# Block-contiguous rows, paired one-hot comparison and shared gather tiles for sixteen ranges in a two-layer graph network

## The chip, the cores and the metric

The kernel runs on one core of one Trainium2 chip. The metric is device time in microseconds (us); a run's time is that of the core, and the kernel before took 14195.87 us, the median of three runs (14195.01 to 14202.4). About 0.2% is what a measurement of this kernel can tell from no change.

## The reference

There are 32768 nodes with 128 features and 524288 edges, sorted by destination. Layer 0 sums neighbours, attends inside groups of 512 nodes, and passes a small network with batch norms. Layer 1 makes three rounds; each sums neighbours again. Cut to what matters here:

```python
# layer 0
agg = jax.ops.segment_sum(x[src], dst, num_segments=N)
h = (1.0 + eps) * x + agg
h = relu(h @ W_loc1 + b_loc1) @ W_loc2 + b_loc2
h_local = _bn(x + h, g1, beta1)
...                                  # attention of 64 groups x 512 nodes, 8 heads of 16
h = h_local + _bn(x + o, g2, beta2)
f = relu(h @ Wf1 + bf1) @ Wf2 + bf2
x = _layernorm(x + _bn(h + f, g3, beta3))
# layer 1, three times (row = src, col = dst)
attn = softmax(x @ Wq.T @ keys.T)    # 512 keys
norm_x = dinv[:, None] * x
agg = zeros_like(x).at[row].add(norm_x[col])
lap = x - dinv[:, None] * agg
x = 0.5 * x + 0.5 * (attn @ values - 0.2 * lap)
# then layer norms and the output
```

The cost lies in the four neighbour sums: one in layer 0 and three in layer 1. Each sends one row of 128 values along each of 524288 edges.

## The kernel before, in words

**Ranges, slots, overflow.** The nodes are cut into 256 ranges of 128 (`NW`). Between each pair of ranges there are `KS = 6` slots for edges. A neighbour sum has two halves. In the first half the sending range multiplies its rows by a one-hot matrix `pick` and so places each row into its slot (`Exchange.spread`, L1406-L1419: matmul `exp`, copy to `y_o` by ScalarE or VectorE, DMA to `slots`). In the second half the receiving range loads its slots (`y_i`, L1424), builds a one-hot matrix `oh` of 19 column groups on VectorE (`Exchange.hot`, L1438-L1442), and adds 19 matmuls into one PSUM tile (`Exchange.add`, L1453). Values are carried as three bf16 parts of 128 each, a row of 384 bf16 elements (768 bytes; 772 bytes in layer 0's table, which has two more columns).

Edges that find no slot are the overflow. Per range, `OW = 5` tiles of 128 rows are gathered by GpSimd with indirect DMAs from the table `rows` (`listed`, L1429), with row numbers from the tensor `other`. What overflows these goes to `SH = 2` tiles of gathered rows shared by `GW = 8` ranges (`common`, L1429 too, asked for at L1434 when `i % GW == 0`, row numbers from `shared`). So one neighbour sum issues 256 x 5 + 32 x 2 = 1344 indirect DMAs of 128 rows. If an overflow did not fit, a flag would lead to a general path (`layer0_any`, `layer1_any`) that is not run here.

**Stages**, with where they lie in the profile:

- Attention of layer 0 (0 to about 3530 us). VectorE also sorts the edges and builds the tensors `slot`, `other`, `shared`, `row` in pieces between attention steps (`Grid.build` L543, `Grid.build_more` L809). The loop at L2122 gives these pieces a quota of 3.35 us of declared cost (`SHARE`) per attention step; each `yield` declares the cost of a piece.
- First half of layer 0's sum (L1741-L1749, about 3530 to 4530 us).
- Second half of it together with the network of `local` (L1802, 4533 to 6235 us). The order is written out by hand (`manual_schedule`). `Sums` (L1455) asks for the gathers and slots six ranges ahead, in seven buffers, and builds one-hots two ahead.
- The second network (L1841, to about 6490 us).
- First half of layer 1's first sum with its softmax (L2039-L2056, about 6490 to 7960 us).
- Two rounds in which each block of four ranges has both the second half of one sum and the first half of the next (L2063-L2082, 7969 to about 10198 us, and on to about 12470 us). `Sums` there builds its one-hots one ahead and compares with `gc["iota1"]`, which lies in SBUF.
- The last second half with the final layer norms (L2086-L2096, 12477 to 14199 us), again in an order by hand. Here and in layer 0's second half `oh` compares with a copy of the ramp in PSUM (`ramp_in_psum`, L1320), in fp32.

**Block tensors.** `rows_of(t, i)` (L1316) views a block of 512 nodes as `[128, 4, d]`: partition `p` holds nodes `p`, `128 + p`, `256 + p`, `384 + p`. A DMA of a block of fp32 features thus moves pieces of 512 bytes, and one of the table `rows` pieces of 768. It is used for the inputs and the output, for the table (`end`, L1361), for `part_d` (what a round adds to the sum: written at L1958, read at L1984), and for `x_d` of round 0 (written at L1891, read at L1988).

**One-hots.** At L1440 the slot number of each of 19 columns is one bf16 element, repeated 128 times along the row by a step of 0, compared with a ramp of 128.

Of the kernel before, what the change touches and what calls it, by code (L numbers as in the profile page):

```python
# [10 lines left out]
I32 = mybir.dt.int32  # L11
# [18 lines left out]
KS = 6  # L30
OV = 6
OW = 5
GW = 8
SH = 2
WL = 2304
BIN = 1024
# [372 lines left out]
                                ordt.rearrange("p t c -> p (t c)"))  # L409


class Grid:


# [128 lines left out]
    def build(self, pp):  # L543
# [9 lines left out]
        with tc.tile_pool(name="gr", bufs=1) as sp:  # L553
# [13 lines left out]
            for h in range(2):  # L567
                with tc.tile_pool(name=f"gr_h{h}", bufs=1) as hp:
# [89 lines left out]
                    with tc.tile_pool(name=f"gr_c{h}", bufs=1) as ap:  # L658
# [19 lines left out]
                        for t, n in ((0, 3), (3, OW - 3)):  # L678
# [5 lines left out]
                        nc.vector.tensor_scalar(key, lw, OS, 7, op0=OP.logical_shift_right,  # L684
                                                op1=OP.logical_shift_left)
                        yield two / 3
                        nc.vector.tensor_scalar(m, lw, main.oth, P - 1, op0=OP.logical_shift_right,
                                                op1=OP.bitwise_and)
                        yield two / 3
                        nc.vector.tensor_tensor(m, m, key, OP.bitwise_or)  # L690
                        yield one / 3
                        nc.vector.tensor_copy(fb[:, :OL], m)
                        yield two / 3
                        nc.vector.tensor_tensor(fb[:, :OL], fb[:, :OL], valid, OP.mult)
# [114 lines left out]
    def build_more(self, lane, pp):  # L809
# [12 lines left out]
        with tc.tile_pool(name="mo", bufs=1) as sp:  # L822
# [10 lines left out]
            for h in range(2):  # L833
                word = words[h]
                m = sp.tile([P, L], I32, name="m")
                n = sp.tile([P, L], I32, name="n")
                valid = sp.tile([P, L], F32, name="valid")
                val = sp.tile([P, L], F32, name="val")
                sz = sp.tile([P, 1], F32, name="sz")
                w = sp.tile([P, 1], F32, name="w")  # L840
                nc.vector.tensor_scalar(w, over.lane_f, float(h * P + 2), None, op0=OP.add)
                nc.vector.tensor_scalar(m, word, over.WSHIFT, None, op0=OP.logical_shift_right)
                yield L / 1000
                nc.vector.tensor_scalar(valid, m, w, None, op0=OP.is_equal, op1=OP.add, accum_out=sz)
# [13 lines left out]
                yield L / 1000  # L858
                nc.vector.tensor_scalar(m, m, 7, None, op0=OP.logical_shift_left)
                yield L / 1000  # L860
                nc.vector.tensor_scalar(n, word, over.oth, P - 1, op0=OP.logical_shift_right, op1=OP.bitwise_and)
                yield L / 1000
                nc.vector.tensor_tensor(m, m, n, OP.bitwise_or)
                yield L / 1000
                nc.vector.tensor_tensor(val, m, valid, OP.mult)
                yield L / 1000
                for t, c in ((0, 3), (3, OW - 3)):
                    yield from self.turned(pp, [val[:, (t + j) * P:(t + j + 1) * P] for j in range(c)],
                                other[:, h, :, t:t + c].rearrange("e w t -> e t w"))
                yield from self.share(pp, sp, keys, val[:, OW * P:OL], sz, self.bad[:, self.NBAD - 2 + h:self.NBAD - 1 + h],  # L870
                           slot[:, OW:, h, :], shared[:, h])
# [18 lines left out]
def tile_gnn_resnorm(ctx: ExitStack, tc: tile.TileContext, a: dict, out: bass.AP):  # L890
# [417 lines left out]
    def grid_consts(pool):  # L1308
        gc["iota1"] = pool.tile([P, P], BF16, name="iota1")
        nc.vector.tensor_scalar(gc["iota1"], iota, 1.0, None, op0=OP.add)  # L1310
        gc["lane1"] = pool.tile([P, 1], F32, name="lane1")
        nc.vector.tensor_scalar(gc["lane1"], lane_f, 1.0, None, op0=OP.add)
        gc["ident"] = pool.tile([P, P], BF16, name="ident_b")
        nc.vector.tensor_copy(gc["ident"], ident)

    def rows_of(t, i):  # L1316

        return t.rearrange("(b c p) d -> b p c d", c=NCH, p=P)[i]

    def ramp_in_psum(pool):  # L1320

        t = pool.tile([P, P], F32, name="ramp_p")
        nc.vector.tensor_copy(t, gc["iota1"])
        return t

    class Exchange:
# [14 lines left out]
            nc.sync.dma_start(self.row.rearrange("p h f -> p (h f)"), self.grid["row"])  # L1341

        def load_tables(self, pool):
            self.slot = pool.tile([P, NC2, NW], BF16, name="slot")
            nc.sync.dma_start(self.slot.rearrange("p c w -> p (c w)"), self.grid["slot"])
            self.other = pool.tile([P, NW, OW], I32, name="other")
            nc.scalar.dma_start(self.other.rearrange("p w c -> p (w c)"), self.grid["other"])
            self.shared = pool.tile([P, NW // GW, SH], I32, name="shared")
            nc.scalar.dma_start(self.shared.rearrange("p g c -> p (g c)"), self.grid["shared"])

        def split_steps(self, wp, b, x, rest):
# [6 lines left out]

            def end():
                nc.vector.tensor_sub(r[:, :, 2, :], rest, r[:, :, 1, :])  # L1360
                nc.sync.dma_start(rows_of(self.table, b), t)  # L1361
            return t[:, :, :ROW], [lambda: nc.scalar.copy(r[:, :, 0, :], x),
                                   lambda: nc.vector.tensor_sub(rest, x, r[:, :, 0, :]),
                                   lambda: nc.scalar.copy(r[:, :, 1, :], rest), end]
# [72 lines left out]

        def hot(self, wp, i, ramp, bufs):  # L1438
            oh = wp.tile([P, NC2, P], BF16, name="oh", bufs=bufs)
            nc.vector.tensor_tensor(oh, ramp[:, None, :].to_broadcast([P, NC2, P]),  # L1440
                                    self.slot[:, :, i].unsqueeze(2).to_broadcast([P, NC2, P]), OP.is_equal)
            return oh  # L1442

        def add(self, ps, oh, got, k):
# [412 lines left out]
    def layer1_grid(v_d, s3, c3):  # L1857

        exs = [Exchange("src", slots_d[t % 2], rows_d[t]) for t in range(T_STEPS)]
        with tc.tile_pool(name="l1g", bufs=1) as gp:  # L1860
# [9 lines left out]
            def first(b, st, wp, p_tr):  # L1870
# [17 lines left out]

                def norm():
                    layer_norm(wp, st["x0"], st["x"])  # L1890
                    nc.sync.dma_start(rows_of(xs_d[0], b), st["x"])  # L1891
                return load, [(7, scale), (12, turn), (15, norm)]

            def prepare(t, b, st, wp, p_s, p_tr):
# [25 lines left out]
            def emit(t, b, st, wp, p_e, p_s, p_tr, share):  # L1920
# [30 lines left out]
                def remain():  # L1951
# [3 lines left out]
                    part = wp.tile([P, NCH, D], F32, name="part_o")  # L1955
                    nc.vector.tensor_tensor(part, ps, st["rec"].unsqueeze(2).to_broadcast([P, NCH, D]), OP.mult)
                    nc.vector.scalar_tensor_tensor(part, st["x"], 0.4, part, op0=OP.mult, op1=OP.add)
                    nc.sync.dma_start(rows_of(part_d, b), part)  # L1958

                def spread(n):  # L1960
                    c, m = divmod(n, KS)
# [18 lines left out]
            def ask_part(t, b, wp):  # L1980

                if b < NB:
                    p_i = wp.tile([P, NCH, D], F32, name="part_i", bufs=3)
                    nc.scalar.dma_start(p_i, rows_of(part_d, b))  # L1984
                    parts[b] = [p_i]
                    if t == T_STEPS - 1:
                        x1 = wp.tile([P, NCH, D], F32, name="x1", bufs=3)
                        nc.scalar.dma_start(x1, rows_of(xs_d[0], b))  # L1988
                        parts[b].append(x1)

            def consume(t, b, st, sums, wp, extra=()):
# [186 lines left out]
```

## Time and profile before

| what | value |
|---|---|
| runs: median of 3 | 14195.87 us |
| the profiled execution: its own time / its span | 14201.3 us / 14199.4 us |
| busy: PE (matmul) / VectorE (DVE) / ScalarE (ACT) / GpSimd (POOL) | 12173.8 / 11413.1 / 6658.1 / 6079.5 us |
| one-hots `oh` with the ramp in PSUM | 512 of 2681 ns |
| one-hots `oh` with the ramp in SBUF | 512 of 2683 ns |
| indirect DMAs `listed` / `common` | 5120 of 1118 ns / 256 of 1299 ns |
| shortest and median of all indirect DMAs | 941 and 946 ns |
| copies `y_o` on ACT / DVE | 4224 of 808 ns / 1920 of 954 ns |
| DMA in all | 3602.99 MB in 1640075 packets |

The busy time of PE is modelled and holds pipelined matmuls twice over in part. Idle time of POOL that is put down to "issue" is time for which the profile shows nothing to wait for. The share of the DMA is the mean over the core's 16 DMA engines; as packets of different queues can overlap on an engine, it can pass 1.

### The profile page before, as it was taken

Reading aid. Unit: us, or ns where it says so; the run is one execution under the profiler, and the core shown is the slowest. Engines: PE = TensorE matmul, PEld = TensorE weight load, DVE = VectorE, ACT = ScalarE, POOL = GpSimd, SP = SyncE. Lnnn points to the kernel's source line nnn. Section 1 sums busy time; section 2 is a strip of 40 time slices with the busy share of each in tenths; the row PEclk is TensorE's granted clock in tenths of the full one; section 3 lists DMA queues with packets and bytes.
Section 4 is the critical chain, followed back from the end, with each engine's and each line's share of the span. In section 5 each row is a group of like instructions: output and inputs, shape, how many; then the busy total and the mean of one; then the engine's idle time right before and its main releaser. Section 6 shows DMA issues by size and latency. Waiting matters only on the chain. (4 is left out here: it accounts for less than half of the span.)

```text
span 14199.4 us, 168166 instructions
## 1 busy us (share of the span) xinstructions
PE 12173.8 (86%) x58982; PEld 5828.9 (41%) x58982; DVE 11413.1 (80%) x16677; ACT 6658.1 (47%) x10316; POOL 6079.5 (43%) x5461
## 2 busy tenths in 40 slices
PE   8888888889887888888998799999899999966666
PEld 3232223333333444444444355555455555533333
DVE  7998998776998888877888677777677777778888
ACT  4343444334987111127888566666566666610000
POOL 0000000000001777740000477877688878767777
PEclk9898888888999999999999999999999999987787
DMA  1000000000999999977888899999999999988887
GB/s 40 11 11 17 10 11 12 18 8 33 348 346 348 309 309 309 310 242 261 304 311 308 299 383 385 390 383 383 350 376 386 382 391 381 383 292 285 286 283 256
DMA packets 1640075, 3602.99 MB, mean 254 GB/s; under 512 B 199346, under 2 KB 976466, under 8 KB 1638066
## 3 DMA queue, kind: packets, MB, share of 16 engines
q1 hardware_dynamic: 1165424, 2936.81, 55.6%
q0 software_dynamic: 258752, 533.02, 12.3%
q10 hardware_dynamic: 215042, 122.32, 2.8%
q8 instruction: 465, 7.62, 0.2%
q14 instruction: 392, 3.21, 0.1%
HBM read 2088.45 MB, written 1503.00 MB: 253 GB/s over the span
## 5 line engine op out<-in xcount | busy, mean ns | idle before, releaser
L1429 POOL DMA_INDIRECT listed<-rows,other x5120 | 5725.6, 1118 | 3544.2 <-issue 3151.1
L1416 ACT CAST y_o<-exp 128x768 bf16<-128x768 f32 x4224 | 3224.0, 808 | 1271.9 <-DMA slots<-y_o 627.2
L1411 PE MATMUL exp<-rows,pick 128*128 128x384 bf16 x12288 | 2768.2, 326 | 394.9 <-ACT y_o L1416 289.4
L1453 PEld LDWEIGHTS <-oh 128*128 128x128 bf16 x19456 | 1992.2, 102 | 2648.8 <-issue 1629.8
L1453 PE MATMUL seg<-y_i,oh 128*128 128x384 bf16 x12288 | 2745.0, 349 | 9.3 <-DMA y_i<-slots 9.3
L1416 DVE CAST y_o<-exp 128x768 bf16<-128x768 f32 x1920 | 1830.9, 954 | 687.4 <-PE exp L1411 636.2
L1411 PEld LDWEIGHTS <-pick 128*128 128x128 fp8e4 x12288 | 1185.1, 97 | 2115.5 <-issue 1550.7
L1453 PE MATMUL seg<-listed,oh 128*128 128x384 bf16 (+1 forms) x5120 | 1257.6, 336 | 815.5 <-DMA listed<-rows,other 777.2
L1606 ACT ACTIVATE pT<-s 128x1024 f32<-128x1024 f32 x1024 | 1021.5, 1023 | 1353.7 <-PE s L1602 1351.3
L1586 DVE TENSOR_REDUCE mx<-s 128x2 f32<-128x1024 f32 x1024 | 1204.4, 1219 | 270.5 <-PE s L1580 270.2
L1440 DVE TENSOR_TENSOR oh<-ramp_p,slot 128x2432 bf16<-128x2432 f32 x512 | 1372.3, 2681 | 12.7 <-DMA slot<-slot_dst 9.4
L1440 DVE TENSOR_TENSOR oh<-iota,slot 128x2432 bf16<-128x2432 bf16 x512 | 1373.7, 2683 | 3.0 <-DMA slots<-y_o 3.0
L283 POOL DMA_INDIRECT c_r<-pivots_over,c_ix x2 | 1.9, 946 | 3056.7 <-DVE c_ix L281 3056.4
L1602 PE MATMUL s<-ql,k 32*128 32x512 f32 x4096 | 1032.4, 692 | 259.2 <-DVE mx L1586 244.6
L2005 DVE SCALAR_TENSOR_TENSOR part_i<-seg,dinv,part_i 128x128 f32<-128x128 f32 x1536 | 529.6, 345 | 543.0 <-PE seg L1453 531.9
L1064 ACT ACTIVATE ln_rs<-ln_mv,eps_c 128x4 f32<-128x4 f32 x192 | 57.1, 297 | 1670.8 <-DVE ln_mv L1062 1489.7
L1930 PE MATMUL s<-keysT,qT 128*128 128x512 f32 x1536 | 818.2, 615 | 7.3 <-ACT pr L1043 3.7
L1453 PE MATMUL seg<-common,oh 128*128 128x384 bf16 (+1 forms) x2048 | 600.7, 350 | 194.5 <-DMA common<-rows,shared 194.2
L1942 PE MATMUL s<-pt,values 128*128 128x512 f32 x1536 | 750.6, 600 | 10.8 <-ACT pt L1937 10.6
L1580 PE MATMUL s<-k,q 32*128 32x512 f32 x4096 | 745.2, 726 | 6.0 <-DVE mx L1586 2.6
L1613 PE MATMUL pv<-pT,vx 128*32 128x512 f32 x4096 | 698.6, 751 | 0.2 <-ACT pT L1606 0.2
L1388 PE MATMUL row_p<-row,ident_b 128*128 128x512 bf16 x1536 | 601.8, 392 | 82.9 <-DVE pick L1381 62.3
(393 smaller groups left out, 14180.8 us busy)
## 6 DMA issues: line engine op xcount, KB each, us to landing
slots<-y_o SPq DMA_DIRECT2D x2048, 576.0 KB
y_i<-slots SPq DMA_DIRECT2D x1024, 1152.0 KB
pick<-pick SPq DMA_DIRECT2D x1024, 192.0 KB
listed<-rows,other POOLq DMA_INDIRECT x5120
rows<-rows SPq DMA_DIRECT2D x192, 384.0 KB
part_d<-part_o SPq DMA_DIRECT2D x192, 256.0 KB
part_i<-part_d ACTq DMA_DIRECT2D x192, 256.0 KB
rows<-rows SPq DMA_DIRECT2D x64, 386.0 KB
```

The costliest lines, as they stand in the source:

```text
L1411: nc.tensor.matmul(ps[:, j, :ROW], pick[:, o:o + P], r, start=True, stop=True)
L1416: (nc.vector.tensor_copy if to_dve else nc.scalar.copy)(dst, ps[:, :, :ROW])
L1429: nc.gpsimd.indirect_dma_start(out=g[:, k, :], out_offset=None, in_=self.table, in_offset=bass.IndirectOffsetOnAxis(ap=index[:, k:k + 1], ...
L1440: nc.vector.tensor_tensor(oh, ramp[:, None, :].to_broadcast([P, NC2, P]), self.slot[:, :, i].unsqueeze(2).to_broadcast([P, NC2, P]), OP.is ...
L1453: nc.tensor.matmul(ps[:, :n], oh[:, j, :], src, start=(k == 0), stop=(k == NC2 - 1))
L1580: nc.tensor.matmul(two[s // 2][:, s % 2, :], t["q", o][32 * s:32 * s + 32, c * P:(c + 1) * P], t["k", o][32 * s:32 * s + 32, :], start=Tru ...
L1586: nc.vector.tensor_reduce(m[:, c, 2 * i:2 * i + 2, xr[o]], st[b]["two"][i], AX.X, OP.max, negate=True)
L1602: nc.tensor.matmul(two[s // 2][:, s % 2, :], t["k", o][32 * s:32 * s + 32, c * P:(c + 1) * P], t["ql", o][32 * s:32 * s + 32, :], start=Tr ...
L1606: nc.scalar.activation(t["p", c][:, 2 * i:2 * i + 2, :], two[i], AF.Exp)
L1613: nc.tensor.matmul(t["o"][32 * s:32 * s + 32, :], t["v"][:, c, s, 2 * o:2 * o + 2, :].rearrange("p z e -> p (z e)"), t["p", c][:, s, :], s ...
L1930: nc.tensor.matmul(s, st["q"][:, c * P:(c + 1) * P], keysT, start=True, stop=True)
L1942: nc.tensor.matmul(ps, values[:, k, :], st["pt"][:, k, :], start=(k == 0), stop=(k == NCH - 1))
```

## The change

- `GW` becomes 16: the two shared tiles serve sixteen ranges, so they are asked for 16 times per sum, not 32 times.
- `kept_of(t, i)` stores the four rows that partition `p` of a block's tile holds side by side, as rows `4p` to `4p + 3` of that block of the tensor, so that one partition's part is one contiguous piece. It replaces `rows_of` for the tables `rows`, for `part_d` and for `x_d` of round 0, but not for inputs and output. The row numbers in `other` and `shared` follow the new order: `row_index` computes them, with six operations where two stood.
- `load_tables` loads `slot` into a tile of its own, and two VectorE copies per load turn it into a tensor `[P, NW, NC2, 2]` in which each element stands twice, side by side. It is loaded twice, for layer 0's second half and at the start of layer 1.
- `hot` compares in pairs: the innermost dimension of all three operands has two neighbouring elements.
- The ramp in PSUM becomes bf16, written by a TensorE transpose of `gc["down"]`.

```diff
-GW = 8
+GW = 16
...
+def row_index(nc, dst, spare, window, lane):
+    n = NCH.bit_length() - 1
+    cost = dst.shape[-1] / 1000
+    lane(dst)
+    yield cost
+    nc.vector.tensor_scalar(dst, dst, n, None, op0=OP.logical_shift_left)
+    yield cost
+    nc.vector.tensor_scalar(spare, window, 7, NCH - 1, op0=OP.logical_shift_right, op1=OP.bitwise_and)
+    yield cost
+    nc.vector.tensor_tensor(dst, dst, spare, OP.bitwise_or)
+    yield cost
+    nc.vector.tensor_scalar(spare, window, 7 + n, 7 + n, op0=OP.logical_shift_right, op1=OP.logical_shift_left)
+    yield cost
+    nc.vector.tensor_tensor(dst, dst, spare, OP.bitwise_or)
+    yield cost
...
-                        nc.vector.tensor_scalar(m, lw, main.oth, P - 1, op0=OP.logical_shift_right,
-                                                op1=OP.bitwise_and)
-                        yield two / 3
-                        nc.vector.tensor_tensor(m, m, key, OP.bitwise_or)
-                        yield one / 3
+                        yield from row_index(
+                            nc, m, fb[:, :OL].bitcast(I32), key,
+                            lambda t: nc.vector.tensor_scalar(t, lw, main.oth, P - 1, op0=OP.logical_shift_right,
+                                                              op1=OP.bitwise_and))
...
+        gc["down"] = pool.tile([P, P], BF16, name="down")
+        nc.vector.tensor_copy(gc["down"], gc["lane1"].to_broadcast([P, P]))
...
+    def kept_of(t, i):
+        return t.rearrange("(b p c) d -> b p (c d)", c=NCH, p=P)[i]
...
     def ramp_in_psum(pool):
-        t = pool.tile([P, P], F32, name="ramp_p")
-        nc.vector.tensor_copy(t, gc["iota1"])
+        t = pool.tile([P, P], BF16, name="ramp_p")
+        nc.tensor.transpose(t, gc["down"], gc["ident"])
         return t
...
-            self.slot = pool.tile([P, NC2, NW], BF16, name="slot")
-            nc.sync.dma_start(self.slot.rearrange("p c w -> p (c w)"), self.grid["slot"])
+            self.slot = pool.tile([P, NW, NC2, 2], BF16, name="slot")
+            with tc.tile_pool(name="slot_l", bufs=1) as lp:
+                t = lp.tile([P, NC2, NW], BF16, name="slot_1")
+                nc.sync.dma_start(t.rearrange("p c w -> p (c w)"), self.grid["slot"])
+                for o in range(2):
+                    nc.vector.tensor_copy(self.slot[:, :, :, o], t.rearrange("p c w -> p w c"))
...
-                nc.sync.dma_start(rows_of(self.table, b), t)
+                nc.sync.dma_start(kept_of(self.table, b), flat(t))
...
-            nc.vector.tensor_tensor(oh, ramp[:, None, :].to_broadcast([P, NC2, P]),
-                                    self.slot[:, :, i].unsqueeze(2).to_broadcast([P, NC2, P]), OP.is_equal)
+            nc.vector.tensor_tensor(oh.rearrange("p c (w z) -> p c w z", z=2),
+                                    ramp.rearrange("p (w z) -> p w z", z=2)[:, None].to_broadcast([P, NC2, P // 2, 2]),
+                                    self.slot[:, i].unsqueeze(2).to_broadcast([P, NC2, P // 2, 2]), OP.is_equal)
...
-                    nc.sync.dma_start(rows_of(part_d, b), part)
+                    nc.sync.dma_start(kept_of(part_d, b), flat(part))
...
-                    nc.scalar.dma_start(p_i, rows_of(part_d, b))
+                    nc.scalar.dma_start(flat(p_i), kept_of(part_d, b))
...
-                        nc.scalar.dma_start(x1, rows_of(xs_d[0], b))
+                        nc.scalar.dma_start(flat(x1), kept_of(xs_d[0], b))
```

The same replacement by `row_index` stands in `build_more` (L861-L865), and the same `kept_of` at L1891. `flat` merges the last two dimensions of a tile.

More of the change, by code (lines that the diff above doesn't have):

```diff
@@ L860, in build_more @@
                 yield L / 1000
[L861 to L865, printed above, removed]
+                yield from row_index(
+                    nc, n, val.bitcast(I32), m,
+                    lambda t: nc.vector.tensor_scalar(t, word, over.oth, P - 1, op0=OP.logical_shift_right,
+                                                      op1=OP.bitwise_and))
+                nc.vector.tensor_tensor(val, n, valid, OP.mult)
                 yield L / 1000
@@ L1318, in rows_of, with flat @@
         return t.rearrange("(b c p) d -> b p c d", c=NCH, p=P)[i]
+    def kept_of(t, i):
+        return t.rearrange("(b p c) d -> b p (c d)", c=NCH, p=P)[i]
+    def flat(t):
+        return t.rearrange("p c d -> p (c d)")
     def ramp_in_psum(pool):
-        t = pool.tile([P, P], F32, name="ramp_p")
-        nc.vector.tensor_copy(t, gc["iota1"])
+        t = pool.tile([P, P], BF16, name="ramp_p")
+        nc.tensor.transpose(t, gc["down"], gc["ident"])
         return t
@@ L1890, in norm @@
                     layer_norm(wp, st["x0"], st["x"])
-                    nc.sync.dma_start(rows_of(xs_d[0], b), st["x"])
+                    nc.sync.dma_start(kept_of(xs_d[0], b), flat(st["x"]))
                 return load, [(7, scale), (12, turn), (15, norm)]
```

## The prediction, made before the run

> **What bounds the kernel now.** The time is a chain of stages, so I read busy times by stage first: the stretches of the profile cut at stage borders (columns: stretch, its length, then busy time and instructions of PE, PE's weight loads, DVE, ACT, POOL; the granted clock, the DMA share, GB/s).
>
> ```profile
> 3540.00:4530.00 990.00, 835.23 (x3831) 366.82 (x3828) 924.74 (x1273) 892.27 (x1276) 6.57 (x62) 1.00 0.91 346
> 4543.00:6225.00 1682.00, 1368.94 (x6610) 731.69 (x6611) 1489.59 (x2671) 184.41 (x443) 1270.34 (x1344) 0.93 0.94 308
> 6500.00:7950.00 1450.00, 1299.50 (x5982) 689.35 (x5983) 1250.68 (x2359) 1268.14 (x2100) 0.00 (x0) 0.99 0.85 304
> 7969.00:10160.00 2191.00, 2040.15 (x10341) 1117.96 (x10342) 1577.97 (x2058) 1295.39 (x2148) 1743.74 (x1344) 0.98 1.01 377
> 10198.00:12400.00 2202.00, 2059.41 (x10461) 1129.91 (x10460) 1588.23 (x2077) 1322.41 (x2191) 1747.59 (x1344) 0.99 1.01 379
> 12477.00:14181.00 1704.00, 1096.38 (x4848) 545.10 (x4849) 1381.56 (x2844) 38.73 (x127) 1294.43 (x1344) 0.79 0.86 285
> ```
>
> In the two stages with hand-written order (second and last row) POOL looks only 76% busy. Its order in time says otherwise:
>
> ```profile
> 13299.35 0.95 POOL L1429 DMA_INDIRECT listed<-rows,other  x1 [0.30 <-issue]
> 13300.60 0.94 POOL L1429 DMA_INDIRECT listed<-rows,other  x1 [0.30 <-issue]
> 13301.85 0.95 POOL L1429 DMA_INDIRECT listed<-rows,other  x1 [0.30 <-issue]
> ```
>
> One starts every 1.25 us, 0.95 busy and 0.30 of issue. 1344 x 1.25 = 1680 us, and the stretches are 1682 and 1704 us long: POOL never rests, and it **bounds both stages**. That PE waits 440.6 us there for `listed` (the waits of 12500 to 14100 us) agrees.
>
> In the two rounds (fourth and fifth row) an indirect DMA takes longer:
>
> ```profile
> L1429 POOL DMA_INDIRECT listed<-rows,other x1280 | 1637.4, 1279 | 2171.4 <-issue 2071.2 <-PE seg L1453 54.2 <-PE exp L1411 20.8
> L1429 POOL DMA_INDIRECT common<-rows,shared x64 | 107.0, 1671 | 20.1 <-issue 16.1 <-PE seg L1453 2.8 <-PE exp L1411 1.2
> ```
>
> The timeline shows why, first POOL's and then DVE's:
>
> ```profile
> 9004.28 0.95 POOL L1429 DMA_INDIRECT listed<-rows,other  x1 [0.30 <-issue]
> 9005.53 3.40 POOL L1429 DMA_INDIRECT listed<-rows,other  x1 [0.30 <-issue]
> 9009.23 0.95 POOL L1429 DMA_INDIRECT listed<-rows,other  x1 [0.30 <-issue]
> ```
>
> ```profile
> 9005.42 2.68 DVE L1440 TENSOR_TENSOR oh<-iota,slot 128x2432 bf16<-128x2432 bf16 x1
> ```
>
> A one-hot whose two inputs lie in SBUF holds POOL's instruction until it is done. Over a round that is 1743.7 - 1344 x 0.946 = 472 us. POOL's demand is thus 1680 + 472 = 2152 of 2191 us. But the DMA engines are full too:
>
> ```profile
> q1 hardware_dynamic: 112714, 317.11, 82.3%
> q0 software_dynamic: 29405, 60.29, 16.9%
> q10 hardware_dynamic: 15312, 7.60, 2.6%
> ```
>
> These are the DMA queues from 8500 to 9500 us (packets, MB, share of 16 engines): 101.8% together. Counting in the trace's DMA records how many packets are open at each moment of 8100 to 10100 us, I find 16 or more for 92% of the time and 13 to 15 for most of the rest; in the last stage only 58%. ACT waits 279.4 us (8000 to 10150 us) for a write of `slots` before it may reuse `y_o`. So I hold the **DMA engines for the bound of the rounds**, POOL 2% behind. PE's floor is 88% of a round (start-to-start: 0.162 us for a matmul of 384 columns, 0.43 for a pass of an fp32 one of 512, 0.109 for a transpose).
>
> [...] The records of 8100 to 10100 us agree: 512 B take 27.0 ns (q10: 27.5), 768 B 36.0, 1536 B 65.5, 4608 B 187.0, so about 6 ns plus 25 B/ns.
>
> **The change part by part**, from the profiled execution: its span of 14199.4 us, 14201.3 with what lies around it, 5 us above the median.
>
> *GW = 16.* Each sum loses 32 of 1344 indirect DMAs: 32 x 1.25 = 40 us of POOL. Layer 0's second half and the last stage: **-40 each**, on the path. What is late next there: DMA, 0.94 and 0.86 busy, and DVE, 0.89 and 0.81, which the one-hots relieve. I counted on the inputs that sixteen ranges need at most 173 (by destination) and 180 (by source) of the 256 shared rows, so the general path isn't taken.
>
> *One-hots in pairs.* [...] 1.27 us x 256 = 324 us of DVE per sum. On the path: **0**, for DVE bounds none of the four stages with one-hots; POOL or the DMA covers it. In the rounds POOL's hold shrinks with it, from 472 to 472 x 1415 / 2681 = 249 us; hidden behind the DMA engines. If that cover is gone, a round gets worth more (rival A). If PSUM keeps 2681 ns, nothing changes on the path.
>
> *Rows side by side.* Per block and partition: four packets of 768 B (144 ns) become one of 3072 B (126, between the 1536 and 4608 B rows), and four of 512 B (108 and 110) become one of 2048 B (86), written and read. 18 + 22 + 24 = 64 ns x 128 partitions / 16 engines x 64 blocks = 33 us per round. With 32 fewer gathers (each 202 + 72 + 9 ns per engine: 9 us) 42 us per round on the bound itself. With POOL and DVE relieved, the engines may run a little fuller (20 us windows reach 1.05): I take **-50 each** round, bounds -35 and -85. In layer 1's first half the same saves about 31 us of DMA work, but the engines are at 0.85 and PE, DVE, ACT at 0.86 to 0.90: -5 (0 to -25). In layer 0's first half 772 B rows save 11 us of DMA, with DVE at 0.93: -3 (0 to -11).
>
> *Loading the slots.* Two copies of 256 x 19 = 4864 bf16, read 512 B apart and written 4 B apart. No row shows one. [...] In layer 0's second half (from 4533 us) slots land at 4540.5, and the first gather starts at 4542.7; behind the copies on DVE stand the first one-hots, behind these PE. PE may start late, since POOL has seven buffers (37 gathers, 46 us) to fill. [...] buffers laid over the loading tile wait: **+8** (0 to 20). At the start of layer 1 (6490 us) DVE's next work is at 6501, and PE, ACT, DVE are all near full after it: **+10** (0 to 20).
>
> *`row_index`.* Per half three more `tensor_scalar` and one more `tensor_tensor`: for 768 columns 3 x 0.54 + 0.95 (scaled from 943 to 1351 and 1749 to 2547 ns for 1536 and 2304) = 2.6 us, for 896 columns 2.9; twice each, 11 us of DVE in the attention stage. There a group of 512 takes 39 us without sorting work and 50 to 75 with it (times between `stats_w`), so DVE is on the path: of DVE's 2946 us in the stage the attention's own rows sum to 1556, and the other 1390 lengthen it by 3530 - 64 x 39 = 1034 us. 11 x 0.74 = **+8** (0 to 15). The declared costs rise by 14 us, or four steps of about 9 us; sorting ended at 3374 of 3530 us, so there is room.
>
> *The new ramp*: two transposes; 0.
>
> Sum: -40 + 8 (layer 0's second half), -3, -5 + 10, -50 - 50, -40, +8 = **-162**; 14201.3 - 162 = 14039, and against the median **14034**.
>
> **The rivals.** *A: the rounds are bound by POOL, not the DMA.* For: POOL idles only 38 us beyond its issue gaps in a round. Against: packets are always queued. POOL's floor would be 1640 + 249 = 1890, PE's about 1950; the fullest 20 us windows move 411 GB/s, and 823 MB at that rate take 2002 us: -189 each in place of -50. 14034 - 278 = **13756**.
>
> *B, slower: the faster one-hot holds POOL also with the ramp in PSUM.* At 2681 ns it doesn't (945 ns per gather), [...] no trace shows the paired mode. If it held POOL as the SBUF form does (0.69 of its length), 0.98 us x 256 = 250 us in each of two POOL-bound stages: 14034 + 500 = **14534**. It decides from a hold of 0.32 us per one-hot (162 / 512).
>
> *C: POOL's bound gives way to the next one.* If in both POOL-bound stages landing gathers take over halfway (-20 each), the rounds gain only 25 each and loads cost 20 each: -20 -20 -25 -25 +40 +8 -3 -5 = -50, **14146**.
>
> *D: the pairs don't engage.* DVE keeps its 2681 ns, and the forecast stays: **14034**, as it rests on POOL and DMA.
>
> **How the numbers follow.** Forecast (with D) 0.67, A 0.10, B 0.07, C 0.16. Forecast's own range: 13950 to 14100. Leaving out A and B and a tail: 13930 to 14150. Faster by over 0.2% (28 us, about what this kernel's measurement can tell from no change): forecast, A and most of C, 0.90; same 0.03; slower B and a bad C, 0.07.
>
> **What would show it.** `common` x128 in all; indirect DMAs still 1.25 us apart in the hand-ordered stages, which shrink by about 40 us; `oh` near 1415 ns in SBUF, 1415 or 2681 in PSUM; long gathers near 1.9 us, not 3.4; rounds 50 us shorter with a DMA share still above 1; packets of 3072 and 2048 B near 126 and 86 ns. I am wrong if rounds shrink by over 100 us, if gathers in the hand-ordered stages pass 1 us, or if a load of slots costs over 20 us.

## The result and the profile after

The changed kernel took 13944.75 us, the median of four runs (13941.91 to 13967.72); the kernel before took 14197.09 us beside it. The ratio is 0.982 with a 95% interval of 0.9807 to 0.9834: 252 us less, where 162 were forecast. The profiled execution took 13967.7 us (span 13965.9), 233.6 us less than that of before and 23 us more than its own median. Cut at the same events in both traces, near the end of each stage, the stages are:

| stage | before, us | after, us | difference | forecast |
|---|---|---|---|---|
| attention with the sorting | 3530 | 3533 | +3 | +8 |
| layer 0, first half | 999 | 994 | -6 | -3 |
| layer 0, second half | 1702 | 1669 | -33 | -32 |
| second network | 257 | 260 | +3 | 0 |
| layer 1, first half | 1475 | 1488 | +13 | +5 |
| round 1 | 2235 | 2143 | -92 | -50 |
| round 2 | 2272 | 2185 | -88 | -50 |
| last second half | 1729 | 1695 | -34 | -40 |

The stretches of the kernel after, with the columns that the prediction explains (length; busy time and instructions of PE, weight loads, DVE, ACT, POOL; clock, DMA share, GB/s):

```profile
3540.00:4527.00 987.00, 837.58 (x3837) 367.61 (x3836) 926.70 (x1277) 892.05 (x1277) 6.63 (x62) 1.00 0.90 348
4538.00:6190.00 1652.00, 1348.52 (x6618) 719.55 (x6619) 1203.72 (x2675) 184.49 (x443) 1246.80 (x1312) 0.95 0.93 312
6467.00:7930.00 1463.00, 1299.96 (x5982) 689.81 (x5983) 1257.11 (x2361) 1269.37 (x2100) 0.00 (x0) 0.99 0.83 302
7949.00:10040.00 2091.00, 2002.48 (x10324) 1123.74 (x10325) 1268.54 (x2055) 1295.02 (x2145) 1382.11 (x1312) 0.99 1.02 393
10122.00:12196.00 2074.00, 1996.62 (x10317) 1120.38 (x10316) 1269.69 (x2057) 1297.12 (x2149) 1353.28 (x1284) 1.00 1.02 396
12277.00:13946.00 1669.00, 1096.07 (x4848) 544.55 (x4849) 1065.49 (x2848) 38.73 (x127) 1267.47 (x1312) 0.80 0.85 289
```

In the second and last row POOL now has 1312 indirect DMAs instead of 1344. At 1.25 us each they are 1640 us, and the stretches are 12 and 29 us longer than that (before 2 and 24 us longer than 1680): POOL still bounds both. Its order in time in the last stage is the same as before:

```profile
13099.42 0.95 POOL L1461 DMA_INDIRECT listed<-rows,other  x1 [0.30 <-issue]
13100.67 0.94 POOL L1461 DMA_INDIRECT listed<-rows,other  x1 [0.30 <-issue]
13101.92 0.95 POOL L1461 DMA_INDIRECT listed<-rows,other  x1 [0.30 <-issue]
```

In the first round (fourth row) POOL is busy for 1382 us of 2091, where before it was 1744 of 2191. The groups of instructions (busy us, mean ns, idle before):

```profile
L1472 DVE TENSOR_TENSOR oh<-iota,slot 128x2432 bf16<-128x2432 bf16 x512 | 724.1, 1414 | 3.0 <-DMA slots<-y_o 3.0
L1472 DVE TENSOR_TENSOR oh<-ramp_p,slot 128x2432 bf16<-128x2432 bf16 x512 | 723.6, 1414 | 3.4 <-DMA slots<-y_o 3.3
L1461 POOL DMA_INDIRECT common<-rows,shared x128 | 123.4, 964 | 39.1 <-issue 36.3 <-PE tr L1987 1.6 <-DMA listed<-rows,other 0.6
L1377 DVE COPY slot<-slot 128x4864 bf16<-128x4864 bf16 x4 | 22.2, 5599 | 7.2 <-DMA slot<-slot_src 4.1 <-DMA slots<-y_o 3.1
```

Both forms of the one-hot take 1414 ns; the copies of the slots take 5.6 us each. The timelines of POOL and DVE in round 1 show the shorter hold, 2.00 us beside a one-hot where before it was 3.40:

```profile
9008.94 0.95 POOL L1461 DMA_INDIRECT listed<-rows,other  x1 [0.30 <-issue]
9010.20 2.00 POOL L1461 DMA_INDIRECT listed<-rows,other  x1 [0.30 <-issue]
```

```profile
9009.96 1.42 DVE L1472 TENSOR_TENSOR oh<-iota,slot 128x2432 bf16<-128x2432 bf16 x1
```

The DMA queues from 8500 to 9500 us (packets, MB, share of 16 engines) carry more bytes than before in fewer packets, and their share is as high:

```profile
q1 hardware_dynamic: 93821, 328.93, 83.2%
q0 software_dynamic: 29695, 60.84, 17.1%
q10 hardware_dynamic: 4320, 7.87, 2.1%
```

### The profile page after: what moved, and what is told of

Read it like the earlier page. It is cut to its first block, busy times and chain, and to the rows that moved or that the text cites. A ratio compares the mean times of both kernels' runs of the same rounds, so it can differ in the third digit from the quotient of the medians.

```text
span 13965.9 us, 167858 instructions
## 1 busy us (share of the span) xinstructions
PE 12092.4 (87%) x58984; PEld 5828.0 (42%) x58984; DVE 10213.4 (73%) x16696; ACT 6660.0 (48%) x10316; POOL 5298.0 (38%) x5333
## 5 line engine op out<-in xcount | busy, mean ns | idle before, releaser
L1461 POOL DMA_INDIRECT listed<-rows,other x5120 | 5153.1, 1006 | 4132.7 <-issue 3151.6
L1486 PE MATMUL seg<-y_i,oh 128*128 128x384 bf16 x12288 | 2652.2, 347 | 21.1 <-DMA y_i<-slots 20.8
L1486 PE MATMUL seg<-listed,oh 128*128 128x384 bf16 (+1 forms) x5120 | 1309.2, 335 | 873.3 <-DMA listed<-rows,other 855.7
L1431 DVE TENSOR_SCALAR_CACHE_REDUCE pick<-row_p,lane 128x512 fp8e4<-128x512 f32 x768 | 556.3, 746 | 259.1 <-PE row_p L1420 245.2
L1472 DVE TENSOR_TENSOR oh<-iota,slot 128x2432 bf16<-128x2432 bf16 x512 | 724.1, 1414 | 3.0 <-DMA slots<-y_o 3.0
L1472 DVE TENSOR_TENSOR oh<-ramp_p,slot 128x2432 bf16<-128x2432 bf16 x512 | 723.6, 1414 | 3.4 <-DMA slots<-y_o 3.3
L1486 PE MATMUL seg<-common,oh 128*128 128x384 bf16 (+1 forms) x2048 | 631.9, 351 | 86.9 <-DMA common<-rows,shared 86.9
```

The source lines that it names most:

```text
L1461: nc.gpsimd.indirect_dma_start(out=g[:, k, :], out_offset=None, in_=self.table, in_offset=bass.IndirectOffsetOnAxis(ap=index[:, k:k + 1], ...
L1472: nc.vector.tensor_tensor(oh.rearrange("p c (w z) -> p c w z", z=2), ramp.rearrange("p (w z) -> p w z", z=2)[:, None].to_broadcast([P, NC2 ...
L1486: nc.tensor.matmul(ps[:, :n], oh[:, j, :], src, start=(k == 0), stop=(k == NC2 - 1))
```

## The experiments

The two stages that POOL bounds gained about what was forecast; the rounds gained nearly twice as much as forecast. So the question was which bound the rounds have. Theory 1 is the prediction's: the DMA engines alone; the pairs bring nothing there. Theory 2 (rival A): POOL, held by the one-hots. Theory 3: a joint bound, in which the pairs' shorter hold on POOL lets the other parts pay in full.

To understand the numbers one needs to know that the runs were spread over chips of two kinds: on the first the kernel before takes 14196 to 14204 us, as in the result; on the second 15006 to 15119 us. The second kind was met on two chips: one for the first four rows below, the other for a_again to b_more_dma and again, less than an hour later, for the last two rows. That other chip gave both ends of the range, 15118.55 and 15006.45 us, so times and ratios of its two groups of runs can be set side by side only roughly. Ratios hold against before on the same chip; runs marked "same" shared the chip of the row above.

| run | chip: before, us | this, us | ratio, 95% interval |
|---|---|---|---|
| b_gw16 | second: 15005.85 | 14886.71 | 0.9921 (0.9907 to 0.9934) |
| b_pairs | same | 15076.25 | 1.0045 (1.0032 to 1.0059) |
| b_kept | same | 15014.65 | 1.0007 (1.0000 to 1.0014) |
| a_unpair | same | 14877.08 | 0.9916 (0.9903 to 0.9930) |
| a_again | second: 15118.55 | 15087.51 | 0.9978 (0.9967 to 0.9988) |
| a_own_tile | same | 15091.95 | 0.9979 (0.9972 to 0.9986) |
| a_more_dma | same | 15126.50 | 1.0004 (0.9994 to 1.0014) |
| b_more_dma | same | 15229.16 | 1.0071 (1.0057 to 1.0086) |
| b_pairs_2 | first: 14203.62 | 14225.42 | 1.0015 (1.0008 to 1.0022) |
| a_more_pe | same | 14123.36 | 0.9938 (0.9925 to 0.9952) |
| a_unpair_2 | second: 15006.45 | 14885.15 | 0.9915 (0.9901 to 0.9928) |
| a_more_dma_2 | same | 15117.33 | 1.0077 (1.0063 to 1.0090) |

### One part alone, on the second kind of chip

**b_gw16**, the kernel before with one line changed:

```diff
-GW = 8
+GW = 16
```

> The kernel before with sixteen ranges per pair of shared tiles and nothing else. Theory 1 (the DMA engines bound the rounds, POOL the two hand-ordered stages): 32 fewer gathers are worth 40 us in each of the two POOL-bound stages and 9 us of DMA work in each round, together about -98 us. Theory 2 (POOL bounds the rounds too): -40 us in all four stages with gathers, about -160 us.

**b_pairs**, the kernel before with the paired one-hots, the doubled slot table and the bf16 ramp:

```diff
-            nc.vector.tensor_tensor(oh, ramp[:, None, :].to_broadcast([P, NC2, P]),
-                                    self.slot[:, :, i].unsqueeze(2).to_broadcast([P, NC2, P]), OP.is_equal)
+            nc.vector.tensor_tensor(oh.rearrange("p c (w z) -> p c w z", z=2),
+                                    ramp.rearrange("p (w z) -> p w z", z=2)[:, None].to_broadcast([P, NC2, P // 2, 2]),
+                                    self.slot[:, i].unsqueeze(2).to_broadcast([P, NC2, P // 2, 2]), OP.is_equal)
```

> The kernel before with one-hots compared in pairs (with the doubled slot tensor and the bf16 ramp) and nothing else. Theory 1: the DMA work of a round is unchanged, so the rounds keep their time within 10 us each; loading the slots costs 13 us at the start of layer 1 and nothing in layer 0; in all between -10 and +20 us. Theory 2: POOL's hold falls from 472 to some 140 us per round, and each round gets about 90 us shorter; in all about -170 us. Theory 3 (POOL and DMA bound the rounds jointly, each within 2% of the other, and their irregularities add up): each round gains 20 to 50 us; in all -30 to -90 us.

**b_kept**, the kernel before with the side-by-side rows and `row_index` alone:

```diff
-                nc.sync.dma_start(rows_of(self.table, b), t)
+                nc.sync.dma_start(kept_of(self.table, b), flat(t))
```

> The kernel before with the rows of a partition side by side (and the new row numbers) and nothing else. Theory 1: -33 us of DMA work per round, -6 in layer 0's first half, +3 in the attention stage; in all about -69 us. Theory 2: the rounds keep their time; in all between -5 and +5 us. Theory 3: each round gains 15 to 30 us.

**a_unpair**, the changed kernel with the one-hots of before, which is GW = 16 and the side-by-side rows together (the diff of b_pairs backwards):

> The changed kernel with the one-hots as before (one element repeated, fp32 ramp in PSUM, slots loaded once). Theory 1: keeps -42 us per round and -40 us in each POOL-bound stage, and saves the loading of the slots: about -165 us against the kernel before. Theory 2: POOL needs 1640 + 472 = 2112 us per round, so the rounds gain 40 us each by the gathers: -160 us too. Theory 3: less than 40 us per round, in all -110 to -150 us.

Measured: -119 us, +70, +9 and -129. No theory foretold all four: theory 1 had said -98, -10 to +20, -69 and -165. Only a_unpair came as one of them said (theory 3), and b_kept within 4 us (theory 2). GW = 16 carries nearly all of the gain. Before left no trace on this chip, but b_kept took about as long and did: against it b_gw16's layer 0 second half is 43 us shorter (1962 for 2005), its last stage 41 (1938 for 1979), its two rounds together 52 (4722.2 for 4774.6). The rows alone bring nothing there. The pairs cost, and more than the loads of the slots explain (layer 1's first half is 12 us longer than in b_kept, 1488 for 1476). What makes this chip 800 us slower is looked at below.

### The whole and the loading tile

**a_again** is the changed kernel, unaltered.

> The changed kernel once more, unaltered, on the chip of this batch, so that its parts can be set against the whole on one chip. Theory 1 (GW=16 and the side-by-side rows are worth what they are worth by themselves, the pairs nothing): about -160 against before. Theory 3 (the rounds have a joint bound, and the pairs' shorter hold on POOL lets GW and the side-by-side rows pay in full): about -230 to -260. On a chip as slow as that of the first batch (before at 15006 us), where pairs alone cost +70 us and everything but the pairs saved 129 us, the sum of the parts would be -60 to -130.

Measured: -31 us. That is less than the -60 to -130 expected of such a chip, and near the sum of the parts as measured on the other chip of this kind, -119 + 70 + 9 = -40. So, as far as two chips can be compared, the parts add up there, with no gain from their meeting, and the gain of the result did not come.

**a_own_tile** keeps the loading tile of the slots in the tables' own pool:

```diff
-            with tc.tile_pool(name="slot_l", bufs=1) as lp:
-                t = lp.tile([P, NC2, NW], BF16, name="slot_1")
...
+            t = pool.tile([P, NC2, NW], BF16, name="slot_1")
```

> The changed kernel with the tile into which the slot table is loaded kept in the tables' own pool, so that nothing allocated after it reuses its memory. If the first stage of layer 1 is 13 us longer because the loads into the reused memory wait for the copies that read the tile: that stage goes from 1488 back to about 1475 us, the whole is 10 to 15 us (0.1%) shorter than the changed kernel. If the 13 us are the copies themselves on VectorE (4 x 5.6 us for two loads): no difference, within 3 us.

The wait is seen in the timeline of the changed kernel at the start of layer 1, on the chip of the result (SP issues the loads, DVE copies):

```profile
6457.35 0.32 SPq L1375 DMA_DIRECT2D slot<-slot_src  x1
6462.96 11.12 DVE L1377 COPY slot<-slot 128x4864 bf16<-128x4864 bf16 x2 [4.09 <-DMA slot<-slot_src]
6474.11 0.80 SPq L1406 DMA_DIRECT2D pick<-pick  x2
```

SP's first `pick` is issued 16.8 us after the load, behind the copies, and with it all that SP issues later. If it goes into memory that the loading tile held, it has to wait for the copies that read that tile. With the tile kept apart, layer 1's first half went from 1491 us (a_again) to 1477, 14 us, and SP's waits there for the load and the copies (5.2 and 11.2 us in a_again) are gone. The stage agrees with the first branch. In the whole the 14 us are not seen (the two medians differ by 4 us, and 0.9979 lies in the other's interval), for the other stages vary by as much on this chip. So the mechanism is shown, a better kernel is not.

### More work for one resource

**a_more_dma** and **b_more_dma** write 256 KB more per block in each round:

```diff
                     nc.sync.dma_start(kept_of(part_d, b), flat(part))
+                    if t:
+                        nc.sync.dma_start(more_d[b], part.rearrange("p c d -> p (c d)"))
```

> The changed kernel with 256 KB more written per block in each round of layer 1 (64 blocks, 128 packets of 2048 B each, into memory that nobody reads): 64 x 128 x 84.4 ns / 16 engines = 43 us of DMA work per round, 86 us in both. If DMA is the bound of the rounds after the change: +75 to +95 us against the changed kernel, nearly all of it in the two rounds. If TensorE or another compute engine bounds them now: under +25 us.

> The kernel before with the same 256 KB more per block in each round. If DMA alone was the bound of the rounds (theory 1, on which the prediction's 42 us of saved DMA work per round rest): +75 to +95 us against before. If POOL, held by the one-hots, was the bound (theory 2): under +25 us. If both together set the pace (theory 3): in between, and less than the changed kernel loses by it.

Measured: +39 us against a_again (the two intervals leave some 20 us either way), +111 against before. Before pays more than the whole 86 us, the changed kernel less than half. That fits theory 1 for the kernel before, and speaks against it for the kernel after, but it is no proof. All of it is measured on the second kind of chip. And the writes are spread evenly over the two rounds, while the loss is not: in the profiled execution of a_more_dma, 52 us above its median, round 1 is as long as in a_again (2448 and 2451 us) and round 2 is 85 us longer (2540 and 2455).

**b_pairs_2** is b_pairs on a chip of the first kind:

> The kernel before with the paired one-hots alone (doubled slot table, 16-bit ramp), once more, on another chip. If before takes about 14196 us on it: theory 1 (DMA alone bounds the rounds) expects +10 to +20 us (the loads of the slot table) and rounds as long as before, 2235 and 2272; theory 2 (POOL, held 472 us a round, bounds them) -100 to -250 us; theory 3 (a joint bound) -40 to -100 us, all of it in the rounds. If before takes 15000 us or more on it, as on the first chip that this kernel was tried on: +50 to +90 us, as there.

Measured: +22 us. The rounds are 2225 and 2286 us (before 2235 and 2272): no gain. Their stretches, and POOL's waits in them:

```profile
7985.00:10157.00 2172.00, 2029.75 (x10363) 1125.78 (x10362) 1273.96 (x2061) 1300.15 (x2155) 1388.55 (x1337) 0.99 1.01 380
10206.00:12416.00 2210.00, 2050.71 (x10451) 1136.41 (x10451) 1285.16 (x2078) 1319.17 (x2187) 1385.46 (x1336) 0.99 1.01 377
```

```profile
POOL listed L1436 <- PE seg L1461: 794.2, 279, 21.8
```

The hold on POOL fell from 472 to 124 us in round 1, DVE's work by 300, and both now wait (POOL 794 us in the two rounds, for the matmuls that free its buffers; before it was 109). So theory 2 falls, and theory 3 too in the form that the pairs alone are worth 40 to 100 us. Theory 1 came within 2 us. But the waiting of PE changed its place: in the two rounds PE waited 9 us for slots to land (`y_i`) before and 104 us here, and for gathers and `y_o` together 252 us before and 162 here. In the changed kernel these are 21 and 143 us. So it isn't excluded that the pairs are worth something beside the other parts.

**a_more_pe** adds TensorE work that changes no sum, in all four stages with gathers:

```diff
+            if k == 0:
+                for _ in range(2):
+                    nc.tensor.matmul(ps[:, :n], oh[:, j, :], src, start=True, stop=True)
             nc.tensor.matmul(ps[:, :n], oh[:, j, :], src, start=(k == 0), stop=(k == NC2 - 1))
```

> The changed kernel in which the first matmul of every segment sum is issued three times instead of once (each of the two more is overwritten by the next, so the sums stay as they are): 256 x 2 matmuls of 385 columns, 0.16 us each on a free TensorE, 82 us of TensorE work in each of the four stages with gathers, 328 us in all. If before takes about 14196 us on the chip: l0 second and last are bound by POOL's gathers and lose under 15 us each, the rounds (TensorE 92 percent) lose 20 to 60 us each, the sum is +50 to +140. If before takes 15000 us or more: theory A, TensorE is what is slow on such a chip (its results come a median 0.5 to 0.9 us later than its records say, up to 10 us) and bounds all four stages, so +280 to +400; theory B, POOL, the DMA engines or the semaphores are what is slow there, so under +140.

```profile
4540.00:6184.00 1644.00, 1397.29 (x7087) 760.01 (x7089) 1214.27 (x2660) 183.68 (x441) 1237.74 (x1306) 0.96 0.94 314
7963.00:10163.00 2200.00, 2059.38 (x10905) 1192.00 (x10905) 1274.98 (x2070) 1326.40 (x2167) 1270.92 (x1301) 0.98 1.00 375
10199.00:12382.00 2183.00, 2061.09 (x10973) 1194.78 (x10972) 1284.55 (x2081) 1342.49 (x2196) 1275.46 (x1304) 0.99 1.01 382
12452.00:14114.00 1662.00, 1124.67 (x5369) 574.91 (x5369) 1063.36 (x2845) 38.04 (x127) 1258.30 (x1310) 0.85 0.86 289
```

The two stages by hand lost nothing (1661 and 1688 us; 1669 and 1695 in the changed kernel, whose chip may be another one of the first kind): POOL bounds them, and 82 us of TensorE vanish. The rounds lost 101 and 70 us, more than the 20 to 60 expected: all of the 82 on average. The whole is 179 us above the changed kernel's 13945, where +50 to +140 was expected. And the DMA share of the rounds is still 1.00 and 1.01, with not one byte more. The packet records say how: a 4608-byte packet took 187.0 and 187.2 ns in the rounds of the changed kernel and 194.5 and 192.6 here. **The recorded time of a packet is no fixed price**: in the two stages by hand of the changed kernel it was 203 and 213 ns, at shares of 0.93 and 0.85. So a share near 1 is no proof of a bound. The same matmuls were not added to the kernel before; whether its rounds would have lost as much is not known.

**a_unpair_2** and **a_more_dma_2** are a_unpair and a_more_dma once more. The chip was of the second kind, the one of a_again:

> The changed kernel with the one-hots of the kernel before (so GW=16 and the side-by-side rows without the pairs), once more, on another chip. If before takes about 14196 us on it, where the pairs alone measured +22 us: if the pairs have no part in the gain of the rounds, -250 to -290 us against before, the rounds at 2130 to 2160 and 2170 to 2200 us with POOL still held some 470 us in each; if the rounds' gain needs the pairs' shorter hold on POOL (theory 3), the rounds stay above 2180 and 2220 us and the whole is -110 to -190 us. If before takes 15000 us or more: -110 to -150 us, as on the first such chip.

> The changed kernel with 256 KB more written per block in each round, once more, on another chip: 43 us of DMA work per round, 86 us in all. If before takes about 14196 us on the chip, where 82 us more of TensorE work per round cost 101 and 70 us: if the DMA engines too bound the rounds (share 1.02 to 1.03 of their time), +60 to +95 us against the changed kernel's 13945 us, 30 to 48 in each round; if TensorE alone bounds them now, under +25 us in both together. If before takes 15000 us or more: +10 to +60 us, as on the second chip of that kind.

Measured: -121 us, as the first time, and +111 against before. The second has no run of the changed kernel beside it. By a_again's time (15088 us) it lost 30 us, by a_again's ratio of 0.9978 some 145, where a_more_dma lost 39. It decides nothing, and leaves the 39 us less sure.

### What is slow on the second kind of chip

The median times of single instructions are the same there (a_again: gathers 949 ns, `oh` 1416 for 1414 to 1415 in the changed kernel's result); the stages without gathers are too (attention 3509 us, layer 0 first half 997). The stages with gathers are 250 to 310 us longer each. A timeline of a_again in layer 0's second half:

```profile
4861.15 0.38 PE L1420 MATMUL row_p<-row,ident_b 128*128 128x512 bf16 x1
4861.36 1.30 PE L1486 MATMUL seg<-y_i,oh 128*128 128x384 bf16 x7
...
4865.16 0.75 DVE L1431 TENSOR_SCALAR_CACHE_REDUCE pick<-row_p,lane 128x512 fp8e4<-128x512 f32 x1 [1.28 <-remote]
4865.43 0.95 POOL L1461 DMA_INDIRECT listed<-rows,other  x1 [2.43 <-remote]
...
4865.98 0.58 PE L1420 MATMUL row_p<-row,ident_b 128*128 128x512 bf16 x1 [2.31 <-DVE pick L1431]
```

By its records PE had finished one range's sum at 4862.66 and four matmuls of the next at 4863.67, and DVE its one-hot at 4863.88. Yet DVE and POOL, whose next instructions wait for PE's semaphore, went on only at 4865.16 and 4865.43. The trace's semaphore events show none of PE's between 4861.53 and 4864.36, and then ten from 4865.07 to 4865.48, 0.03 to 0.08 us apart, while these matmuls start 0.16 us apart. Over the stages of b_gw16, PE's next recorded signal comes over 0.5 us after the matmul's end for about a half, a quarter, a quarter and a half of the matmuls that signal in the four stages with gathers, and for 0% in the four without; in before, after, b_pairs_2 and a_more_pe for 0% everywhere. The shares are rough, for in those four stages the trace of b_gw16 holds only 9538 of the 12427 signals that its matmuls give (in the others all of them). So on the second kind the **signals come late and in bursts**, and only in the stages with indirect DMAs. That the indirect DMAs are the cause is not shown. Why it is so, and why the pairs cost there (rounds of 4823 us for 4775 of b_kept on one chip, 4906 in a_again for 4741 in a_unpair_2 on the other), stays open.

## Why the prediction was right, and where a term was off

The gain is 252 us where 162 were forecast; 13945 us lies 5 us below the forecast's own range of 13950 to 14100 and inside its outer one. In the table of stages the surplus is in the rounds alone: -180 us for -100. All other stages together make -54 for -62.

**GW = 16: -40 in each stage bound by POOL.** Right in kind: -33 (with +8 for the slots, forecast -32) and -34 (forecast -40). That -33 meets -32 is partly luck: b_pairs_2 loads the slots in the same way, and its layer 0 second half takes 1702 us as before, so the +8 is not seen and the gathers brought some 34 instead of 40 in both stages. It isn't the pairs: alone they left these stages at 1702 and 1730 us (before 1702 and 1729). The bound was read from the spacing of the instructions, not from a share, and held in every run on the first kind of chip, a_more_pe's 82 us included.

**One-hots: 1415 ns, 0 on the path.** Right: 1414 ns in both forms, with the ramp in PSUM as with it in SBUF (before 2681 and 2683). The 1415 ns was the author's estimate; no trace of before has a one-hot in pairs. 0 on the path is shown by b_pairs_2 for the pairs alone. The hold was taken to fall in proportion to the one-hot's length, from 472 to 249 us, and fell to 141 in round 1. That step was wrong. In the rounds of both kernels a gather that meets a one-hot ends 0.82 us (median) after it, so what it loses is the rest of the one-hot, and this gets shorter by the whole 1.27 us. For 256 one-hots that is 325 us, and 472 - 325 = 147 (an estimate, for not every one-hot meets a gather). Rival B did not come: the median gather in the stages by hand takes 0.949 us (before 0.946), and all that gathers of the last stage take beyond 0.946 us is 26 us (before 24). Only the very first one in layer 0's second half was held, to 4.37 us, beside the slot copies: it ended at 4542.74, they at 4541.91.

**Rounds: -50 each, bounds -35 to -85.** The term that was mis-sized: -92 and -88, beyond its bounds. The sign and the 42 us of DMA work hold, as far as the records tell; the other half of the gain has no term in the prediction but "the engines may run a little fuller". Three things are measured in its place.

- DMA work. 42 us per round were forecast. The sum of all packets' time, over 16 engines, fell by 73 us in round 1 (2242 to 2169) and 68 in round 2. The new packets cost what was estimated (121.7 ns for 3072 bytes, 85.7 for 2048; forecast 126 and 86). Of the 73 us, some 30 are 4608-byte packets getting cheaper (190.2 to 187.0 ns, 151000 / 16 of them), so about 42 are left. But a_more_pe shows that such a sum is partly an outcome of how long the round takes, so what fuller engines would bring cannot be worked out from it.
- TensorE. With the prediction's start-to-start times its floor is 1923 and 1971 us before, 1927 and 1968 after: unchanged. What is beyond the floor fell from 312 and 301 us to 216 and 217. In b_pairs_2 it stayed at 298 and 318; in a_more_pe the floor rose to 2006 and 2055 and the rest stayed at 238 and 200. So after the change a round is TensorE's floor plus some 200 to 240 us of waiting, and the change took its gain out of the waiting.
- Part of that waiting may come from SP. It issues the `slots` and `y_i` transfers and stands behind earlier ones. The waits of SP's queue for a landing `part_i`, both rounds (us, times, longest), before and then after:

```profile
SPq L1424 <- DMA part_i<-part_d: 374.0, 75, 8.1
SPq L1419 <- DMA part_i<-part_d: 192.8, 35, 8.6
SPq L1374 <- DMA part_i<-part_d: 14.1, 3, 5.1
```

```profile
SPq L1991 <- DMA part_i<-part_d: 124.9, 55, 3.7
SPq L1451 <- DMA part_i<-part_d: 44.0, 15, 4.9
SPq L1456 <- DMA part_i<-part_d: 34.1, 38, 2.2
SPq L1406 <- DMA part_i<-part_d: 3.3, 3, 2.2
```

That is 581 us before and 206 after (617 with the pairs alone). In packets, a load of `part_i` takes a median 9.85 us from issue to its last packet before, 10.48 with the pairs alone, and 6.40 after: one packet of 2048 bytes for four of 512. The prediction had counted packets as engine time only. The about 6 ns per packet that the prediction fitted to the packets' recorded times (27.0 ns for 512 bytes, 187.0 for 4608) are too small for it: 384 packets fewer are 24 per engine, 0.14 us (an estimate from that fit), and the load lands 3.5 us sooner. Why it does stays open. That these waits, and not the 32 gathers fewer, made the other half of the gain is argued, not shown: on the first kind of chip neither part was run alone, and theory 3's version (the pairs needed beside the others) isn't excluded there. One run speaks against it: in a_more_pe, which is the changed kernel too, the trace shows no wait of SP's queue for `part_i` in the rounds, and the time beyond the floor is no shorter (238 and 200 us). On the second kind the load shortened as well (8.48 us in b_gw16, 5.35 in b_kept) and b_kept gained nothing, but its rounds wait for signals.

**"The DMA engines for the bound of the rounds."** For the kernel before, b_pairs_2 takes POOL and DVE off the list, and b_more_dma (+111 us) fits the DMA engines, though on the second kind of chip. It is not shown beyond that. In the changed kernel they are not the only bound: 82 us of TensorE work cost 101 and 70 us (a_more_pe). The prediction gave TensorE, whose floor it had at 88%, no part in the rounds. Whether it had one already before the change was not tested.

**Slots and start of layer 1: +10.** +13 in the stage, +12 in b_pairs_2, and 14 back in a_own_tile. The copies took 11.1 us per load, under the 20 us from which the prediction would have been wrong. The cause is the one that the prediction named for the other load: buffers laid over the loading tile wait.

**Small terms.** The -5 for side-by-side rows in layer 1's first half are not seen (1476 us in b_kept and 1477 in a_unpair, which have the rows without the pairs; before 1475). `row_index` was to cost 8 us and the attention stage differs by 3; it lies between 3509 and 3542 us in all kernels, changed or not, so that is not resolved.

## What to carry to other kernels

A bound read from a fixed spacing of instructions (1.25 us from gather to gather) carried the forecast to within 7 us. A DMA share near 1 did not carry it, since the recorded packet times grew with the time of the round (187.0 to 194.5 ns for 4608 bytes); adding 82 us of work to one engine told more than the share. Where rows are made longer, look at the latency of the loads too (9.85 to 6.40 us here), not at the engines' time alone. Where an instruction is held until another ends, as the gathers beside a one-hot are here, it gains the whole of what the other gets shorter, not a share of it (the hold fell from 472 to 141 us when the one-hot fell from 2683 to 1414 ns). And try a change on more than one chip: the changed kernel gains 1.8% on one kind and 0.2% on the other, where leaving the pairs out gains 0.85%. What leaving them out does on the first kind was not run.

## What was not expected of the hardware

- Two chips can differ by some 6% on one kernel with the same instruction times: 14196 against 15006 to 15119 us, with PE's next recorded signal over 0.5 us late for about half of the signalling matmuls in b_gw16's last stage, and over 8.9 us for a tenth.
- The same 4608-byte packet takes 187 ns in a round of 2143 us and 194.5 in one of 2244.
- A gather beside a one-hot of 1.42 us took 2.00 us, and the hold per round fell from 472 us to 141 (124 with the pairs alone), to under a third, while the one-hot's length fell to 53%.
